# A decoder layer's cross-attention context: joining two token tiles on VectorE before TensorE's sum over partitions, with GpSimd's work of a round put in another order

## Chip, cores and metric

The kernel runs on one NeuronCore of a Trainium2 chip. Its time is the device time of one execution in microseconds (us). The kernel before takes 456.52 us in the median of three runs (455.98 to 457.6).

## What is computed

The reference is one pre-norm decoder layer over 8 batch rows of 256 tokens and 256 features, all in float32. It has three parts, each added to its input: linear self-attention, a cross-attention whose context is one vector for each batch row, and a mixture of 8 experts of which each token takes two. The part that the change touches is the middle one:

```python
def xattn(q, k, v, Wq, Wk, Wv, Wfc):         # k = v = the context, 8 x 256 x 256
    qp = l2norm(q @ Wq)                       # per token, over features
    kp = l2norm(k @ Wk)
    vp = v @ Wv
    kv = jnp.sum(kp * vp, axis=-2, keepdims=True)   # sum over the 256 tokens
    return qp * kv @ Wfc + v
```

The experts' part needs a list of which token goes to which expert. It is made on the chip: each token and choice writes its number and gate into a slot of a table in device memory, and later steps read the table 128 slots at a time.

## The kernel before

**Tiling.** A batch row (`b`, 0 to 7) has 256 tokens, held as T = 2 tiles of 128 partitions, with 256 features along the free axis. Features on partitions come as KD = 2 halves of 128.

**Stages.** The front of the kernel works on rows in a software pipeline. A loop over `i` from 2 to 7 (lines 1072 to 1131) makes one round of each `i`; the round runs stages of row `i` (first norm, queries, keys, context projection), of row `i-1` (self-attention's state, attend, output), of row `i-2` (cross-attention) and of row `i-3` (choice of experts, ranks, table). Rows 0 and 1 have a start written out by hand (lines 1022 to 1069), and rows 6 and 7 an end written out by hand (lines 1135 to 1195), in which the first steps of the experts' matrix products are put between the stages by `meanwhile`. After that only experts' steps are left. A step takes 128 gathered tokens through one expert, some 36 steps in all.

**Order.** TensorE, VectorE, ScalarE and the queue that SyncE issues DMAs from execute in the order of the source. GpSimd's order is chained to the source's by `in_turn` and by the list `behind`. [...] So a stage's place in the loop is its place in every engine's queue, and a wait at the head of a queue holds all that stands behind it.

**The context's sum.** `context` (L388) projects 128 context tokens with `Wk` and `Wv` side by side; ScalarE squares the key half with a running sum (`ssk`), VectorE multiplies the halves (`prod`, L401). After the second tile `inverse_length` computes 1/length on GpSimd: a maximum (L330, tile `l2n_k`) and a power (L309, tile `l2r_k`, named `rn` in the code). `context_sum` (L469) then forms the 256 sums over tokens as matrix products, with `prod` as the weights and the column `rn[:, t]` as the moving operand, accumulated over the two token tiles; a copy by VectorE (L480, `kvc`) takes the result out of PSUM. It shares the PSUM bank of `state` (L453), whose matrix products come before it. `turn_queries` (L556) is the first to use the result, one round later.

**GpSimd's share of a round.** `add_context` (L530) adds the context to the residual for `cross_out`, a 128x512 addition (L536, tile `xc`; in the hand-written end VectorE does it, L534). `residual` (L372) adds the output bias (L374). The two inverse lengths and the inverse roots of the three norms (tiles `rs_a`, `rs`, `rs_b`) are small operations. `place` (L706) ends with four indirect DMAs (L729) that write the table `slots` for one row: two token tiles times two choices.

**Readers of the table.** `fetch_slots` (L850) has SyncE read 128 slots (L853, tile `ids`). In the round `i` = 7 (`i - 3 == RA`) six of these are issued, for steps 3 to 8; in the source they stand behind `place(4)`, and the table is one tensor to the dependency tracker: a read waits for earlier writes, and a write for earlier reads. The gathers of tokens for the experts' steps (`gather`, L871) are GpSimd's too.

Of the kernel before, what the change touches and what calls it, by code (L numbers as in the profile page):

```python
# [13 lines left out]
ALU = mybir.AluOpType  # L14
# [3 lines left out]
P = 128  # L18
# [6 lines left out]
ORDERED = mybir.DependencyInfo(mybir.DependencyClass.NoSync, mybir.DependencyReason.SCHED_ONLY)  # L25
# [4 lines left out]
def decoder_kernel(  # L30
# [34 lines left out]
    nc = tc.nc  # L65
    ctx.enter_context(tc.manual_schedule(engines={ET.PE, ET.SP, ET.DVE, ET.Activation}))
    B, S, D = x.shape
# [3 lines left out]
    T = S // P  # L71
# [16 lines left out]
    slots = dram.tile([NTILE, 2 * P], I32, name="slots")  # L88
# [4 lines left out]
    def ps(name):  # L93
        return psum.tile([P, 512], F32, tag="ps", name=name)
# [4 lines left out]
    def const(name, shape, dtype=F32):  # L99
        return cpool.tile(shape, dtype, tag=name, name=name)  # L100
# [31 lines left out]

    load(0)

    any_w = const("any_w", [P, P])
    nc.vector.memset(any_w, 1.0)
    def idle(n):
        p = ps("idle")
        for _ in range(n):
            nc.tensor.matmul(p[:, 0:P], any_w, any_w, start=True, stop=True)  # L140

    idle(8)
    mhalf = const("mhalf", [P, 2 * T])
# [27 lines left out]
    for i, v in enumerate((gamma, beta)):  # L171
        at = n_b1 + i * KD
# [108 lines left out]
    def gate_row():  # L281
        p = ps("pglog")
        for k in range(KD):
            nc.tensor.matmul(
                p[:, 0:E], beta_w[:, k, :], wg_s[:, k, :], start=(k == 0), stop=(k == KD - 1)
            )
        nc.vector.tensor_copy(glog, p[:, 0:E])


    behind = []  # L290
# [162 lines left out]
    def state(st):  # L453
# [12 lines left out]
            st["kvz"], p, headsx[:, None, :].to_broadcast([P, KD, VW]), ALU.mult  # L466
        )

    def context_sum(st):  # L469

        b = st["b"]
        p = st["pstate"][:, KD * VW : KD * VW + KD]
        for m in range(KD):
            for t in range(T):
                nc.tensor.matmul(
                    p[:, m : m + 1], st["prod"][:, t, m * P : (m + 1) * P], st["rn"][:, t : t + 1],
                    start=(t == 0), stop=(t == T - 1),
                )
        st["kv"] = small.tile([P, KD], F32, tag="kvc", name=f"kvc{b}")
        nc.vector.tensor_copy(st["kv"], p)  # L480

# [134 lines left out]
    puts = []  # L616

    def named(st):

        def new(name, shape, dtype=F32):  # L620
            t = st[name] = small.tile(shape, dtype, tag=name, name=f"{name}{st['b']}")
            return t
        return new
# [82 lines left out]
    def place(st):  # L706

        new = named(st)
        at = st["b"] * T
        hot = st["hot"]  # L710
        slot = new("slot", [P, T, E])
        nc.vector.tensor_tensor(
            slot,
            st["prank"].rearrange("p (t e) -> p t e", e=E),
            slot0[:, None, :].to_broadcast([P, T, E]),
            ALU.add,
        )
        nc.vector.tensor_tensor(
            hot, hot, slot[:, :, None, :].to_broadcast([P, T, 2, E]), ALU.mult
        )  # L720
        pos = new("pos", [P, T, 2])
        nc.vector.tensor_reduce(pos, hot, axis=AX.X, op=ALU.add)
        posi = new("posi", [P, T, 2], I32)
        nc.vector.tensor_copy(posi, pos)
        earlier = list(behind)
        behind.clear()
        for t in range(T):
            for c in range(2):
                put = nc.gpsimd.indirect_dma_start(  # L729
                    out=slot_rows,  # L730
                    out_offset=bass.IndirectOffsetOnAxis(ap=posi[:, t, c : c + 1], axis=0),
                    in_=pay[:, at + t, c, :], in_offset=None,
                )
                tc.declare_no_dep(
                    put.ins, group="slots", reason="every token and choice has a slot of its own"
                )
                tc.add_to_no_dep_group("slots", put.ins)
                for name in earlier:
                    tc.add_manual_dep(put.ins, name, ORDERED, reason="in the order of the source")
                puts.append(put.ins.name)  # L740
                behind.append(put.ins.name)


    w2_s = w2pool.tile([P, E, FC, D], F32, tag="w2", name="w2_s")
# [94 lines left out]
    def said(s, which, engine):  # L839
        top = (E, NTILE)[which] - 1  # L840
        plan, at = (plans["a"], s) if s < NA else (plans["b"], s - NA)
        return nc.values_load(
            plan[0:1, which, at : at + 1], engines=[engine], min_val=0, max_val=top,
            skip_runtime_bounds_check_because=CLAMPED,
        )
# [4 lines left out]
    def fetch_slots(s):  # L850
        q_sp = said(s, 1, ET.SP)
        ids[s] = mpool.tile([P, 2], I32, tag="ids", name=f"ids{s}", bufs=16)
        got = nc.sync.dma_start(ids[s], slot_rows[bass.ds(q_sp * P, P), :])  # L853
        if s in (0, NA):
            for name in puts[0 : RA * T * 2] if s == 0 else puts:
                tc.add_manual_dep(got.ins, name, WRITTEN, reason="all slots are written")

    def fetch_weights(s):
        e_sp = said(s, 0, ET.SP)
        w1s[s] = mpool.tile([P, KD, F], F32, tag="w1", name=f"w1_{s}", bufs=3)  # L860
        nc.sync.dma_start(
            w1s[s], w1_rows[bass.ds(e_sp * D, D), :].rearrange("(k p) f -> p k f", p=P)
        )
        b2s[s] = mpool.tile([P, D], F32, tag="b2", name=f"b2_{s}", bufs=3)
        nc.sync.dma_start(b2s[s], b2_flat[bass.ds(e_sp * D, D)].partition_broadcast(P))
# [5 lines left out]
    def gather(s):  # L871
        xgs[s] = mpool.tile([P, D], F32, tag="xg", name=f"xg{s}", bufs=6)
        in_turn(nc.gpsimd.indirect_dma_start(  # L873
            out=xgs[s][:, :], out_offset=None, in_=rows_d[0 : reach(s), :],
            in_offset=bass.IndirectOffsetOnAxis(ap=ids[s][:, 0:1], axis=0),
        ))
# [129 lines left out]
    def step_end():  # L1006

        at = len(done)
        while len(done) == at:
            next(work)  # L1010
# [4 lines left out]
    def run(stage, b, *args):  # L1015
        if 0 <= b < B:
            stage(rows[b], *args)
# [29 lines left out]


    run(state, 0)
    run(lift_queries, 1)  # L1050
    run(keys, 1, 0)
    run(context_sum, 0)
# [19 lines left out]
    for i in range(2, B):  # L1072
        run(turn_context, i)
        run(turn_normed, i)
        run(choose, i - 3)
        run(state, i - 1)
        run(turn_second, i - 2)
        run(powers, i - 3, False)
        run(add_context, i - 2)
        run(gates, i - 3)  # L1080
        run(first_stats, i + 1)
        run(queries, i)
        run(residual, i)
        run(cross_queries, i - 2)
        run(context_sum, i - 1)
        run(lift_queries, i)
        run(rank, i - 3)
        run(attend, i - 1)
        run(place, i - 3)
        run(first_norm, i + 1)  # L1090
        run(attended, i - 1)
        if i - 3 == RA - 1:
            plan = plan_steps("a", RA - 1, NA, full_tiles)
            next(plan)
        if i - 3 == RA:
            for s in range(3, NA):
                fetch_slots(s)
        run(turn_queries, i - 2)
        run(keys, i, 0)
        if i == 2:  # L1100
            gate_row()
        run(cross_out, i - 2)
        if i == B - 1:
            gather(0)
            gather(1)
        if i - 3 == RA - 1:
            next(plan)
        run(turn_attended, i - 1)
        run(keys, i, 1)
        run(key_powers, i)  # L1110
        run(last_norms, i - 2)
        if i - 3 == RA - 1:
            for _ in plan:
                pass
            for s in range(3):
                fetch_slots(s)
        run(attention_out, i - 1)
        run(second_stats, i - 1)
        run(lift_keys, i)
        run(base, i - 2)  # L1120
        run(context, i, 0)
        run(turn_last, i - 2)
        run(second_norm, i - 1)
        run(context, i, 1)
        run(logits, i - 2)
        if i + 3 < B:
            load(i + 3)
        for e in seconds[i]:
            load_second(e)
        if i - 3 == RA - 1:  # L1130
            fetch_weights(0)
# [3 lines left out]
    p, q = B - 2, B - 1  # L1135
    run(choose, p - 1)
    run(state, q)
    run(turn_second, p)
    run(powers, p - 1, True)
    run(gates, p - 1)  # L1140
    turn(0)
    fetch_weights(1)
    run(cross_queries, p)
    run(rank, p - 1)
    run(context_sum, q)
    meanwhile(0.8)
    run(attend, q)
    run(place, p - 1)
    run(attended, q)
    run(add_context, p, True)  # L1150
    run(turn_queries, p)
# [19 lines left out]
    run(rank, p)  # L1171
    run(gates, p)
    run(place, p)
    run(add_context, q, True)
    holding[0] = True
    meanwhile(1.7)
# [13 lines left out]
    meanwhile(3.5)  # L1190
    run(rank, q)
    run(place, q)
    step_end()
    for _ in plan_steps("b", B - 1, NSTEP - NA, other_tiles):
        pass
# [50 lines left out]
```

## Time and profile before

| what | value |
|---|---|
| median of 3 runs | 456.52 us (455.98 to 457.6) |
| profiled execution | 460.37 us, of which the span from first to last instruction is 458.7 us |
| mean granted TensorE clock | 0.983 |
| busy: TensorE, weight loads, VectorE, ScalarE, GpSimd | 435.1, 374.2, 186.5, 212.3, 187.3 us |
| one round of the loop, from the transposes of row 4's context (94.81 us) to those of row 5's (115.55 us) | 20.74 us |
| `context_sum` in all: matrix products, weight loads (L475) | 64 of 7.7 us; 64 of 8.3 us |
| additions by GpSimd, 128x512: `xc` (L536), bias (L374) | 6 of 1.28 us each; 8 of 1.27 us each |
| table writes (L729), issue by GpSimd | 32 of 1.01 us each, 32.2 us in all, with 9.0 us of idle time before them |

"Busy" is the time in which an engine's instructions run; a matrix product's end is modelled. In a row of the profile the first number is the start in us from the span's start or, in a group, the sum; the bracket behind a row tells how long the engine was idle and what ended that. PE is TensorE's products, PEld its weight loads, DVE VectorE, ACT ScalarE, POOL GpSimd, SPq the queue of SyncE. A float32 product of the source is two in the trace.

### The profile page before, as it was taken

Reading aid. Unit: us, or ns where it says so; the run is one execution under the profiler, and the core shown is the slowest. Engines: PE = TensorE matmul, PEld = TensorE weight load, DVE = VectorE, ACT = ScalarE, POOL = GpSimd, SP = SyncE. Lnnn points to the kernel's source line nnn. Section 1 sums busy time; section 2 is a strip of 40 time slices with the busy share of each in tenths; the row PEclk is TensorE's granted clock in tenths of the full one; section 3 lists DMA queues with packets and bytes.
Section 4 is the critical chain, followed back from the end, with each engine's and each line's share of the span. In section 5 each row is a group of like instructions: output and inputs, shape, how many; then the busy total and the mean of one; then the engine's idle time right before and its main releaser. Section 6 shows DMA issues by size and latency. Waiting matters only on the chain. (4 is left out here: it accounts for less than half of the span.)

```text
span 458.7 us, 8535 instructions
## 1 busy us (share of the span) xinstructions
PE 435.1 (95%) x2679; PEld 374.2 (82%) x2679; DVE 186.5 (41%) x692; ACT 212.3 (46%) x551; POOL 187.3 (41%) x201
## 2 busy tenths in 40 slices
PE   9999999999999999997999999999999999999960
PEld 7568777686878688886999999999999999999950
DVE  1776878787897867361112121111212111121100
ACT  4545546555644455343444444444444444444420
POOL 7323363645546662744342433324243342422220
PEclk9999999999999999998999999999999999999995
DMA  8603268584404256886777667686776767677325
GB/s 228 210 25 115 73 204 111 170 190 126 94 24 129 46 150 228 136 204 118 189 199 236 164 218 191 201 239 152 228 186 202 194 195 238 156 224 197 70 30 191
DMA packets 48368, 74.37 MB, mean 162 GB/s; under 512 B 9773, under 2 KB 37810, under 8 KB 48290
## 3 DMA queue, kind: packets, MB, share of 16 engines
q1 hardware_dynamic: 39298, 63.10, 44.8%
q0 software_dynamic: 8208, 9.91, 14.3%
q10 hardware_dynamic: 816, 0.79, 0.5%
q8 instruction: 24, 0.39, 0.3%
q14 instruction: 22, 0.18, 0.2%
HBM read 64.44 MB, written 11.44 MB: 165 GB/s over the span
## 5 line engine op out<-in xcount | busy, mean ns | idle before, releaser
L902 PEld LDWEIGHTS ph<-xgT,w 128*128 128x128 f32 x1152 | 170.0, 192 | 17.1 <-issue 4.2
L902 PE MATMUL ph<-xgT,w 128*128 128x128 f32 x1152 | 176.1, 276 | 3.3 <-issue 3.2
L906 ACT ACTIVATE hT<-ph,vcols 128x128 f32<-128x128 f32 x288 | 105.3, 367 | 141.8 <-PE ph L902 118.0
L915 PE MATMUL py<-w_s,hT 128*128 x576 | 170.8, 382 | 0.0
L936 POOL DMA_INDIRECT acc<-yg,ids x36 | 57.1, 1586 | 152.5 <-DVE yg L930 129.7
L885 DVE TENSOR_SCALAR xgT<-pt,vcols 128x128 f32<-128x128 f32 x72 | 26.2, 406 | 157.1 <-PE pt L882 156.7
L915 PEld LDWEIGHTS py<-w_s,hT 128*128 128x128 f32 x576 | 88.7, 193 | 0.6
L873 POOL DMA_INDIRECT xg<-rows_d,ids x36 | 36.0, 1001 | 11.2 <-issue 9.6
L930 DVE SCALAR_TENSOR_TENSOR yg<-py,ids,b 128x256 f32<-128x256 f32 x36 | 17.4, 484 | 45.8 <-ACT hT L906 35.5
L729 POOL DMA_INDIRECT slots<-pay,posi x32 | 32.2, 1006 | 9.0 <-issue 8.0
L347 PE MATMUL pxkv<-xwkv_s,cT 128*128 128x512 f32 x64 | 30.1, 593 | 0.0
L347 PE MATMUL pkv<-wkv_s,hT 128*128 128x512 f32 x64 | 29.9, 593 | 0.0
L347 PEld LDWEIGHTS pxkv<-xwkv_s,cT 128*128 128x128 f32 x64 | 11.5, 190 | 8.0 <-issue 7.6
L924 ACT ACTIVATE b<-b,ids 128x256 f32<-128x256 f32 x36 | 17.9, 498 | 0.0
L347 PEld LDWEIGHTS pkv<-wkv_s,hT 128*128 128x128 f32 x64 | 11.1, 190 | 8.2 <-issue 8.1
L309 POOL TENSOR_TENSOR rs_b<-ve_b,mhalf 128x2 f32<-128x2 f32 x8 | 8.2, 1021 | 23.1 <-DVE ve_b L322 23.1
L309 POOL TENSOR_TENSOR rs_a<-ve_a,mhalf 128x2 f32<-128x2 f32 x8 | 5.7, 708 | 27.1 <-DVE ve_a L322 27.1
L347 PEld LDWEIGHTS po<-wo_s,turnedoT 128*128 128x128 f32 x64 | 12.1, 190 | 4.6 <-issue 3.3
L347 PE MATMUL pq<-xwq_s,turnedx2T 128*128 128x256 f32 x64 | 15.2, 381 | 0.5 <-issue 0.5
L511 ACT COPY turnedoT<-pto 128x512 f32<-128x512 f32 x8 | 4.7, 585 | 23.6 <-PE pto L341 21.0
L410 PE MATMUL pq<-hT,wq_s 128*128 128x256 f32 x64 | 15.2, 381 | 0.2 <-ACT hT L386 0.2
L347 PE MATMUL pfc<-xwfc_s,turnedq2T 128*128 128x256 f32 x64 | 15.2, 380 | 0.0
(193 smaller groups left out, 523.2 us busy)
## 6 DMA issues: line engine op xcount, KB each, us to landing
w<-in_L_ffn_W_dram SPq DMA_DIRECT2D x36, 1024.0 KB
w_s<-in_L_ffn_W_dram SPq DMA_DIRECT2D x8, 1024.0 KB
b<-in_L_ffn_b_dram SPq DMA_DIRECT2D x36, 128.0 KB
x<-in_x_dram SPq DMA_DIRECT2D x8, 256.0 KB
rows_d<-h SPq DMA_DIRECT2D x8, 256.0 KB
acc<-x SPq DMA_DIRECT2D x8, 256.0 KB
c<-in_ctx_dram SPq DMA_DIRECT2D x7, 256.0 KB
ids<-slots SPq DMA_DIRECT2D x36, 1.0 KB
```

The costliest lines, as they stand in the source:

```text
L309: in_turn(nc.gpsimd.tensor_tensor(dst, src, mhalf[:, 0:n], ALU.pow))
L347: nc.tensor.matmul(p[:, 0:width], srcT[:, k, t * P : (t + 1) * P], w[:, k, 0:width], start=(k == 0), stop=(k == KD - 1),)
L410: nc.tensor.matmul(p[:, m, :], wq_s[:, k, m * P : (m + 1) * P], st["hT"][:, k, :], start=(k == 0), stop=(k == KD - 1),)
L729: put = nc.gpsimd.indirect_dma_start(out=slot_rows, out_offset=bass.IndirectOffsetOnAxis(ap=posi[:, t, c : c + 1], axis=0), in_=pay[:, at ...
L873: in_turn(nc.gpsimd.indirect_dma_start(out=xgs[s][:, :], out_offset=None, in_=rows_d[0 : reach(s), :], in_offset=bass.IndirectOffsetOnAxis ...
L885: nc.vector.tensor_scalar(ready[s][:, k, :], p[:, k * P : (k + 1) * P], gamma_c[:, k : k + 1], beta_c[:, k : k + 1], op0=ALU.mult, op1=ALU ...
L902: nc.tensor.matmul(p, w1s[s][:, k, c * P : (c + 1) * P], ready[s][:, k, :], start=(k == 0), stop=(k == KD - 1),)
L906: nc.scalar.activation(hT[:, c, :], p, AF.Gelu_apprx_tanh, bias=vcols[:, bass.ds(e_act * FC + c, 1)],)
L915: nc.tensor.matmul(p[:, 0:D], hidden[s][0][:, c, :], w2_flat[:, bass.ds((e_pe * FC + c) * D, D)], start=(c == CHUNKS[0]), stop=(c == CHUNK ...
L924: nc.scalar.activation(b2s[s], b2s[s], AF.Copy, scale=gate_of(s))
L930: nc.vector.scalar_tensor_tensor(yg, p[:, 0:D], gate_of(s), b2s.pop(s), op0=ALU.mult, op1=ALU.add)
L936: in_turn(nc.gpsimd.indirect_dma_start(out=acc[0 : reach(s), :], out_offset=bass.IndirectOffsetOnAxis(ap=ids.pop(s)[:, 0:1], axis=0), in_= ...
```

## The change

A new stage `add_tiles` scales the first product tile by its inverse lengths and adds the second tile times its own, both on VectorE, in place. `context_sum` then needs one product for each half of the features instead of two, with a column of ones (the constant that the idle products at the start used, renamed) as the moving operand.

Stages are moved with it. In the loop `add_tiles` comes straight behind `state`; `context_sum` moves from behind `cross_queries` to before it; `add_context` moves from behind `powers` to behind `lift_queries`, and so, in GpSimd's queue, from behind the context's inverse length to behind the queries' one. The four table writes become a stage `put`: the writes of the first token tile stand behind `place`, those of the second behind `cross_out`, and in the last round (`i` = 7) behind `second_stats`. In the hand-written end `add_tiles` stands before `powers`, and `context_sum` before `cross_queries`.

```diff
+    def add_tiles(st):
+        prod, rn = st["prod"], st["rn"]
+        nc.vector.tensor_scalar_mul(prod[:, 0, :], prod[:, 0, :], rn[:, 0:1])
+        nc.vector.scalar_tensor_tensor(
+            prod[:, 0, :], prod[:, 1, :], rn[:, 1:2], prod[:, 0, :], op0=ALU.mult, op1=ALU.add
+        )
...
         for m in range(KD):
-            for t in range(T):
-                nc.tensor.matmul(
-                    p[:, m : m + 1], st["prod"][:, t, m * P : (m + 1) * P], st["rn"][:, t : t + 1],
-                    start=(t == 0), stop=(t == T - 1),
-                )
+            nc.tensor.matmul(
+                p[:, m : m + 1], st["prod"][:, 0, m * P : (m + 1) * P], ones[:, 0:1],
+                start=True, stop=True,
+            )
...
+    def put(st, *ts):            # the indirect DMAs that ended place()
+        at, posi = st["b"] * T, st["posi"]
         earlier = list(behind)
         behind.clear()
-        for t in range(T):
+        for t in ts or range(T):
...
     run(state, 0)
+    run(add_tiles, 0)
...
         run(state, i - 1)
+        run(add_tiles, i - 1)
         run(turn_second, i - 2)
         run(powers, i - 3, False)
-        run(add_context, i - 2)
         run(gates, i - 3)
         run(first_stats, i + 1)
         run(queries, i)
         run(residual, i)
+        run(context_sum, i - 1)
         run(cross_queries, i - 2)
-        run(context_sum, i - 1)
         run(lift_queries, i)
+        run(add_context, i - 2)
         run(rank, i - 3)
         run(attend, i - 1)
         run(place, i - 3)
+        run(put, i - 3, 0)
...
         run(cross_out, i - 2)
+        if i + 1 < B:
+            run(put, i - 3, 1)
...
         run(second_stats, i - 1)
+        if i + 1 == B:
+            run(put, i - 3, 1)
...
     run(state, q)
     run(turn_second, p)
+    run(add_tiles, q)
     run(powers, p - 1, True)
     run(gates, p - 1)
     turn(0)
     fetch_weights(1)
+    run(context_sum, q)
     run(cross_queries, p)
     run(rank, p - 1)
-    run(context_sum, q)
     meanwhile(0.8)
     run(attend, q)
     run(place, p - 1)
+    run(put, p - 1)
```

More of the change, by code (lines that the diff above doesn't have):

```diff
@@ L133, in decoder_kernel @@
     load(0)
-    any_w = const("any_w", [P, P])
-    nc.vector.memset(any_w, 1.0)
+    ones = const("ones", [P, P])
+    nc.vector.memset(ones, 1.0)
     def idle(n):
@@ L139, in idle @@
         for _ in range(n):
-            nc.tensor.matmul(p[:, 0:P], any_w, any_w, start=True, stop=True)
+            nc.tensor.matmul(p[:, 0:P], ones, ones, start=True, stop=True)
     idle(8)
@@ L724, in place @@
         nc.vector.tensor_copy(posi, pos)
+    def put(st, *ts):
+        at, posi = st["b"] * T, st["posi"]
         earlier = list(behind)
         behind.clear()
-        for t in range(T):
+        for t in ts or range(T):
             for c in range(2):
-                put = nc.gpsimd.indirect_dma_start(
+                ins = nc.gpsimd.indirect_dma_start(
                     out=slot_rows,
@@ L732, in place @@
                     in_=pay[:, at + t, c, :], in_offset=None,
-                )
[L734 to L737, printed above, removed]
+                ).ins
+                tc.declare_no_dep(
+                    ins, group="slots", reason="every token and choice has a slot of its own"
+                )
+                tc.add_to_no_dep_group("slots", ins)
                 for name in earlier:
-                    tc.add_manual_dep(put.ins, name, ORDERED, reason="in the order of the source")
-                puts.append(put.ins.name)
-                behind.append(put.ins.name)
+                    tc.add_manual_dep(ins, name, ORDERED, reason="in the order of the source")
+                puts.append(ins.name)
+                behind.append(ins.name)
     w2_s = w2pool.tile([P, E, FC, D], F32, tag="w2", name="w2_s")
@@ L1173, in decoder_kernel @@
     run(place, p)
+    run(put, p)
     run(add_context, q, True)
@@ L1192, in decoder_kernel @@
     run(place, q)
+    run(put, q)
     step_end()
```

## Prediction

> **What bounds the kernel now.** I read the page first, then busy time by stretches of one round, then the timeline of one round, last the timeline around the round `i` = 7 and the start of the hand-written end.
>
> ```profile
> PE 435.1 (95%) x2679; PEld 374.2 (82%) x2679; DVE 186.5 (41%) x692; ACT 212.3 (46%) x551; POOL 187.3 (41%) x201
> 83.00:104.00 21.00, 20.75 (x108) 15.46 (x107) 16.56 (x66) 11.67 (x30) 11.31 (x14) 1.00 0.67 164
> ```
>
> The second line is one round: TensorE (first number behind the length) is busy 20.75 of 21.00 us, VectorE 16.56, GpSimd 11.31. TensorE is the bound in the rounds and in the experts' steps, so each microsecond that TensorE loses or saves there moves the end. The next fence is the middle of the round of `i` = 5.
>
> ```profile
> 96.02 1.28 POOL L536 TENSOR_TENSOR xc<-x,c 128x512 f32<-128x512 f32 x1
> 96.22 1.11 DVE L645 TENSOR_TENSOR ex<-m 128x16 f32<-128x16 f32 x1
> 98.16 0.43 DVE L465 TENSOR_TENSOR kvz<-pstate,headsx 128x272 f32<-128x272 f32 x1
> 100.55 0.95 PE L475 MATMUL pstate<-l2r_k,prod 128*128 128x1 f32 x8
> 101.36 0.17 PE L698 MATMUL prank<-before,ones_h 128*128 128x16 bf16 x1
> 101.53 0.16 DVE L480 COPY kvc<-pstate 128x2 f32<-128x2 f32 x1 [0.92 <-PE pstate L475]
> 101.75 0.38 PE L490 MATMUL pat<-kvz,qT 128*128 128x136 f32 x1 [0.20 <-DVE kvc L480]
> 104.31 0.81 ACT L561 ACTIVATE turnedq2T<-ptq,kvc 128x256 f32<-128x256 f32 x2
> 104.83 0.19 PEld L347 LDWEIGHTS pfc<-xwfc_s,turnedq2T 128*128 128x128 f32 x1 [0.24 <-ACT turnedq2T L561]
> ```
>
> Three things are to be seen. The context's sum holds TensorE from 100.55 to the next product at 101.36: 0.81 us for 8 products, 0.10 each. VectorE's L645 takes 1.11 us while GpSimd adds `xc` and ends 0.03 us after it; the same instruction takes 0.15 us at 158.48 with no addition beside it. And TensorE is released by VectorE's `kvc` (0.20 us of idle) and, with 0.06 us to spare, by ScalarE's `turnedq2T`, whose first half ends at 104.77. The last place is where the loop meets its end:
>
> ```profile
> 149.01 0.96 POOL L729 DMA_INDIRECT slots<-pay,posi  x1 [0.30 <-issue]
> 154.07 4.55 SPq L853 DMA_DIRECT2D ids<-slots  x6
> 155.12 1.08 POOL L309 TENSOR_TENSOR rs_b<-ve_b,mhalf 128x2 f32<-128x2 f32 x1 [0.37 <-DVE ve_b L322]
> 157.29 0.21 POOL L330 TENSOR_SCALAR l2n_k<-ssk 128x2 f32<-128x2 f32 x1 [1.09 <-ACT junkk L398]
> 157.59 0.72 POOL L309 TENSOR_TENSOR l2r_k<-l2n_k,mhalf 128x2 f32<-128x2 f32 x1
> 158.51 0.38 PE L882 MATMUL pt<-ident,xg 128*128 128x128 f32 x2
> 159.35 1.99 PE L347 MATMUL pq<-xwq_s,turnedx2T 128*128 128x256 f32 x8 [0.46 <-issue]
> 159.51 0.43 DVE L465 TENSOR_TENSOR kvz<-pstate,headsx 128x272 f32<-128x272 f32 x1
> DMA packets 199, 0.06 MB, mean 96 GB/s; under 512 B 144, under 2 KB 199, under 8 KB 199
> DMA packets 194, 0.20 MB, mean 326 GB/s; under 512 B 3, under 2 KB 194, under 8 KB 194
> SPq L853 <- DMA slots<-pay,posi: 13.9, 3, 10.9
> 210.50:213.90 3.40, 3.10 (x12) 2.82 (x13) 0.56 (x2) 0.98 (x3) 0.64 (x1) 0.52 0.89 60
> ```
>
> The last of row 4's four table writes is issued at 149.01. SyncE's six reads of the table wait for it until 154.07 (10.9 us is the longest wait of that line), 5.1 us after that issue. They are issued one every 0.84 us, the sixth at 158.29. The two DMA lines are the stretches 159.2 to 159.8 and 159.8 to 160.4: small packets, which the reads consist of, end with the first, so the last read has landed at about 160. Row 7's `l2n_k` and `l2r_k` run meanwhile, since nothing of the table stands before them in GpSimd's queue. The last line is for the clock, below.
>
> **The change, part by part.** Times are on the clock of the trace before.
>
> *TensorE's products.* 4 of 8 go in each of 8 rows: 4 x 0.10 = 0.40 us a row. `kvc` is now long done when `pat` comes, so its 0.20 us of idle can go too: up to 0.6 us a row.
>
> *VectorE's additions.* `add_tiles` is a TENSOR_SCALAR on 128x256 (nearest row: L313, 0.41 us) and a SCALAR_TENSOR_TENSOR with two operands in SBUF (L449, of that kind, takes 0.685 us at 512 elements; rows of 256 elements with two operands, L401, take 0.42). The second reads the first's result: about 0.8 us a row. In the rounds `i` = 3 to 6, L645 gets 0.96 us back as `xc` leaves, so `kvz` ends at 96.9 to 97.7 and `add_tiles` at about 98.5. TensorE ends `queries` at 98.8. No wait; the cover is L645's lost stall, and without it TensorE would wait 0.7 us.
>
> *GpSimd's order.* Here a rule speaks against the change. The row: L645, with both inputs in SBUF, waits for a 128x512 addition; L424, L501 and L435, with one input in PSUM, don't. The Trainium skill, GPSIMD Engine Reference, section Key points, says that GpSimd shares its SBUF interfaces with VectorE and that contention comes with two SBUF inputs and with VectorE's two-port modes, so single-input copies and scalings too. By the row, the bias addition (now 101.2 to 102.5, since VectorE gets to `rs_a` a little earlier) meets `place`'s product L718, which has two SBUF inputs and comes at 101.6 now that `kvc` no longer waits 0.92 us: it ends at 102.5, and `off`, ScalarE's norm and `turnedq2T` come 0.27 us earlier than before, not 0.6. By the rule also the reciprocals L500 wait, for `xc` at its new place (about 104.0 to 105.3), up to 1.3 us; no row here has one beside such an addition. `o` then ends at 105.7 instead of 104.92, and its transpose begins at 106.77: covered, so the sum is the same. The bound is L561: TensorE's gain stops at 0.3 us a round. Bounds: 0 and 0.6. Rounds 3 to 6: 4 x -0.3 = -1.2 us. Round 2 has no choice of experts and 0.4 us of work between: -0.4 us. Row 0: VectorE's queue to `o` (26.1) is TensorE's limit at 26.4, and the added 0.8 us meets 0.83 us of waits there: -0.1 us.
>
> *The table writes of the second tile* stand behind `rs` in the rounds up to 6: two issues, 1.1 + 0.3 + 1.0 us, from 110.5 to 113.0, before `rs_b` at 113.3. Nothing else waits; cost nothing, with 0.3 us of cover. In round 6 they delay the reads for steps 0 to 2 (137.77) by 2 to 3 us, and weights behind them on SP's queue that TensorE needs at 162: covered.
>
> *Round 7.* VectorE is late here, behind the list of steps that round 6 makes (L788 and others): L645 runs at 138.87, not 0.7 us earlier as in a usual round, and waits for the bias addition, which now comes where `xc` was, to 139.25; L649's 1.14 us stall behind it goes. `kvz` at 140.1, `add_tiles` from 140.4 to 141.3. TensorE is ready for the sum at 140.34: it waits 0.95 us, and is 0.35 us later at `pat` after the products saved and the `kvc` wait. +0.4 us.
>
> *The hold.* In this round the second tile's writes stand behind `second_stats`, while SyncE's six reads stand before them. GpSimd's queue becomes: `rs_b`, write 3, write 4, `l2n_k`, `l2r_k`. Write 3 has to wait until all six reads have landed, as they read the same table, and the reads wait for write 2. With pq2 1.4 us later, `l2r_q` ends at 146.2, `xc` 147.5; writes 1 and 2 are issued at 147.7 and 149.1. Reads from 149.1 + 5.1 to 5.5 = 154.4, the sixth at 158.6, landed at 160.4 (its 1.7 us as before). GpSimd, ready at 156.5, stands for 4 us. Then write 3 and 4 (1.1 + 0.3 + 1.0 + 0.3) to 163.1, `l2n_k` and `l2r_k` (0.3 + 0.7) to 164.2, `add_tiles` (0.8, at the head of VectorE's queue, which it holds) to 165.1. TensorE is done with `turn(0)` at 159.1, and its next instruction is now the sum: it idles 6 us. All experts' products and the last rows' stages stand behind it. Before, its idle time there was 0.62 us (158.73 to 159.35). `cross_queries` starts at 165.5, 6.15 us later, of which 0.35 is round 7's; 0.9 us of products is saved behind `prank`. +4.9 us.
>
> *The clock.* The last line of the fence: after two gaps of 1.9 and 2.1 us at 206 to 210.8, the granted clock is 0.52 for 3.4 us. A gap of 6 us should do the same where TensorE is the bound: 3.4 x 0.48 = +1.6 us. The skill (TensorE: Matmul & The Clock Gate, section HAM oscillation) puts the limit at one idle window of about 3.4 us and the return at a busy one; with the windows badly placed that is two at half rate, 3.3 us. The row is this kernel's own, so 1.6; 0 and 3.3 are the ends.
>
> **Sum:** -0.1 - 0.4 - 1.2 + 0.4 + 4.9 + 1.6 = +5.2 us. The profiled execution took 460.37 us (span 458.7), so 465.6 for a profiled one; the runs shown stand 3.85 us below it at a median of 456.52, and the same difference gives 461.7 us.
>
> **Rivals.**
>
> *GpSimd is not held (not slower).* If the sixth read lands before `rs_b` ends (156.5), write 3 goes at once, its two issues end at 159.1 and `l2r_k` at 160.2, `add_tiles` at 161.0: TensorE waits 1.9 us, 1.3 more than before, less 0.9. Clock untouched. With 0.6 us in each of five rounds, -3.0 - 0.1 + 0.4 + 0.4 = -2.3 us: 454.2. For it: the fetches may be faster than 0.84 us with fewer writes ahead. Against: six issues alone take 4.2 us. 7%; with the usual gains of 0.3, about 455.6 us.
>
> *The hold is longer.* In rounds 3 and 4 the second write landed 9 and 10 us after its issue, beside weight loads, where the later rounds have 5 to 5.7 (the semaphores' updates in the trace). If row 4's takes 9, the reads start 3 to 4 us later and TensorE with them; with two slow clock windows +10 us: 466.5. 18%.
>
> *Every round loses.* If `add_tiles` meets a GpSimd operation and TensorE waits 0.7 us in each of five rounds, nothing is gained there: 5 x (0.7 - 0.3) on top of the hold, +9 us: 465.5. For it: VectorE at 16.6 of 21 us; against: GpSimd is idle from 96.1 to 100.5. 10%.
>
> *As worked out*, 65%: 459 to 464.
>
> **How the numbers follow.** Predicted 461.7 us. The range 457.8 to 466.5 takes in full gains with no slow clock at its low end, the long hold at its high end. 0.3% (1.4 us) is about what a measurement of this kernel can tell from no change. Slower by more than that: the last three cases, less a small part of the first of them: 0.90. Of the 7% and what is over, faster 0.05, no change 0.05.
>
> **What would show it.** Right: in the new trace `l2r_k` of row 7 starts several us after row 7's `ssk`, behind two table writes; VectorE's first `add_tiles` instruction of that row waits for GpSimd; TensorE has one gap of about 6 us near 157 to 163, with a clock near 0.5 after it; L645's group falls from 0.66 us mean to near 0.2; L718's rises; a round takes 20.2 to 20.6 us. Wrong: no gap over 3 us at the start of the end, or rounds longer than 20.7 us.

## The result, and the profile after

The changed kernel takes 462.11 us in the median of four runs (461.92 to 463.55), the kernel before on the same chip 456.38 us (455.98 to 457.6): a ratio of 1.0142, 95% interval 1.0118 to 1.0166 (the two medians alone give 1.0126, inside it). On another chip, later, the same pair stood at 1.0168 (1.0141 to 1.0196). The forecast was 461.7 us.

The profiled execution took 461.92 us, with a span of 460.1, so it lies 0.19 us below its median, where the profiled one of before lay 3.9 us above. Before's profile holds the dip at 206 to 213.9 us that the prediction showed (3.4 us at a clock of 0.52; its two gaps are 1.47 and 1.70 us between products, while the 1.9 and 2.1 us of the prediction are those of the weight loads); the profile after has none there. So the spans differ by only 1.4 us while the medians differ by 5.7: the two traces are compared stage by stage here, not by their spans.

First the round `i` = 5 in the timeline of the kernel after (start, duration, engine, line; the bracket is the idle time before and what ended it). Lines have moved: `ex` is now L652, `add_tiles` L472 and L473, the sum L482, `place`'s product L725, `xc` L543, `turnedq2T` L568, the table writes L740, the reads L864.

```profile
93.92 0.15 DVE L652 TENSOR_TENSOR ex<-m 128x16 f32<-128x16 f32 x1
95.68 0.48 DVE L473 SCALAR_TENSOR_TENSOR prod<-prod,l2r_k 128x256 f32<-128x256 f32 x1
96.52 0.50 PE L482 MATMUL pstate<-ones,prod 128*128 128x1 f32 x4
98.93 1.28 POOL L374 TENSOR_TENSOR x<-x,bo_b 128x512 f32<-128x512 f32 x1
99.24 1.01 DVE L725 TENSOR_TENSOR hot<-hot,slot 128x32 f32<-128x32 f32 x1
101.42 1.27 POOL L543 TENSOR_TENSOR xc<-x,c 128x512 f32<-128x512 f32 x1
101.68 0.25 DVE L507 RECIPROCAL den<-den 128x16 f32<-128x16 f32 x1
101.77 0.81 ACT L568 ACTIVATE turnedq2T<-ptq,kvc 128x256 f32<-128x256 f32 x2
102.28 1.99 PE L347 MATMUL pfc<-xwfc_s,turnedq2T 128*128 128x256 f32 x8 [0.20 <-ACT turnedq2T L568]
```

The sum holds TensorE for 0.36 us (96.52 to the next product at 96.88) instead of 0.81. `ex` is back at 0.15 us, and `add_tiles` ends at 96.16, ahead of the sum. The stall has moved: L725 takes 1.01 us beside the bias addition; before, as L718, it took 0.19:

```profile
102.59 0.19 DVE L718 TENSOR_TENSOR hot<-hot,slot 128x32 f32<-128x32 f32 x1
```

TensorE no longer waits for `kvc` but for ScalarE's `turnedq2T`. The transposes of the context (`ptc`), which open each round, stand at 52.20, 72.37, 92.52 and 112.67 us, against 53.35, 74.09, 94.81 and 115.55: a round takes 20.16 us instead of 20.73. When the round `i` = 7 begins, TensorE is 3.26 us ahead (before, then after):

```profile
136.34 0.64 PE L341 MATMUL ptc<-ident,c 128*128 128x128 f32 x4
133.08 0.64 PE L341 MATMUL ptc<-ident,c 128*128 128x128 f32 x4
```

Then the round `i` = 7 and the start of the hand-written end, from the same timeline (SPq is SyncE's DMA queue; its duration is from the first of six issues to the last):

```profile
138.44 0.61 PE L482 MATMUL pstate<-ones,prod 128*128 128x1 f32 x4 [1.19 <-DVE prod L473]
146.27 0.97 POOL L740 DMA_INDIRECT slots<-pay,posi  x1 [0.30 <-issue]
152.77 4.55 SPq L864 DMA_DIRECT2D ids<-slots  x6
159.66 1.04 POOL L740 DMA_INDIRECT slots<-pay,posi  x1 [6.30 <-DMA ids<-slots]
162.33 0.73 POOL L309 TENSOR_TENSOR l2r_k<-l2n_k,mhalf 128x2 f32<-128x2 f32 x1
163.09 0.35 DVE L472 TENSOR_SCALAR prod<-prod,l2r_k 128x256 f32<-128x256 f32 x1 [5.99 <-POOL l2r_k L309]
164.02 1.01 PE L482 MATMUL pstate<-ones,prod 128*128 128x1 f32 x4 [7.97 <-DVE prod L473]
164.90 3.76 PE L347 MATMUL pq<-xwq_s,turnedx2T 128*128 128x256 f32 x8
```

Read the brackets upward from the sum at 164.02: TensorE stood 7.97 us for `add_tiles`, which stood 5.99 us for `l2r_k`, which came behind two table writes, of which the first stood 6.30 us for the six reads. The last line takes 3.76 us; at full clock it took 1.99. The stretches of that stage show why (length, TensorE's busy time and count, and after ScalarE's and GpSimd's numbers the granted clock):

```profile
157.00:163.00 6.00, 0.00 (x0) 0.00 (x0) 0.10 (x1) 0.00 (x0) 2.92 (x4) 0.81 0.74 231
163.00:166.40 3.40, 2.38 (x8) 2.11 (x9) 2.78 (x13) 0.00 (x0) 1.22 (x2) 0.50 0.96 116
166.40:170.00 3.60, 3.60 (x15) 2.97 (x14) 0.72 (x4) 1.27 (x5) 0.00 (x0) 0.50 0.08 16
```

TensorE runs nothing at all from 157 to 163, and everything behind that at half rate. The next stretch, 170.00 to 173.40, has a clock of 0.86. Counted as time at 0.50 that is 2.3 us inside the gap (6 x 0.19 / 0.5), then 3.4, 3.6 and 0.95 us (3.4 x 0.14 / 0.5): 10.2 us in all, where the prediction had 3.4.

### The profile page after: what moved, and what is told of

It is laid out like the page before. It is cut to its first block, busy times and chain, and to the rows that moved or that the text cites. A ratio compares the mean times of both kernels' runs of the same rounds, so it can differ in the third digit from the quotient of the medians.

```text
span 460.1 us, 8471 instructions
## 1 busy us (share of the span) xinstructions
PE 432.6 (94%) x2647; PEld 371.6 (81%) x2647; DVE 189.6 (41%) x708; ACT 212.3 (46%) x551; POOL 187.7 (41%) x201
## 5 line engine op out<-in xcount | busy, mean ns | idle before, releaser
L740 POOL DMA_INDIRECT slots<-pay,posi x32 | 32.5, 1016 | 16.6 <-issue 7.4
L347 PE MATMUL pq<-xwq_s,turnedx2T 128*128 128x256 f32 x64 | 17.5, 421 | 0.0
L347 PEld LDWEIGHTS pfc<-xwfc_s,turnedq2T 128*128 128x128 f32 x64 | 11.7, 190 | 5.4 <-ACT turnedq2T L568 3.6
L347 PEld LDWEIGHTS po<-wo_s,turnedoT 128*128 128x128 f32 x64 | 12.1, 190 | 4.6 <-issue 3.3
L347 PE MATMUL po<-wo_s,turnedoT 128*128 128x256 f32 x64 | 15.2, 380 | 0.0
```

The source lines that it names most:

```text
L347: nc.tensor.matmul(p[:, 0:width], srcT[:, k, t * P : (t + 1) * P], w[:, k, 0:width], start=(k == 0), stop=(k == KD - 1),)
L740: ins = nc.gpsimd.indirect_dma_start(out=slot_rows, out_offset=bass.IndirectOffsetOnAxis(ap=posi[:, t, c : c + 1], axis=0), in_=pay[:, at ...
```

## The experiments

The theory: the rounds gain 3.3 us; the second tile's late table writes of round 7 hold GpSimd and through it TensorE; the long gap halves the clock; and the sum's early place in the end exposes what is late. The rivals are given with each run. All ratios are to the kernel before, measured on the same chip in the same set. The kernel after itself was run beside e9 and e10 only; a difference between its ratio and that of another experiment, or between e1's and those of e5 and e6, is one between chips.

**e1: both tiles' writes early.** The hold is taken out, all else of the change stays.

```diff
-        run(put, i - 3, 0)
+        if i + 1 < B:
+            run(put, i - 3, 0)
+        else:
+            run(put, i - 3)
...
-        if i + 1 == B:
-            run(put, i - 3, 1)
```

> Only change against the kernel after: in the round i = 7 both tiles' table writes of row 4 are issued behind `place`, as before; `add_tiles`, the halved sum and every other move stay. Theory (the late writes hold GpSimd, and through `l2r_k`, `add_tiles` and the sum TensorE): the wait of the write for the six reads is gone, TensorE's gap at the start of the end shrinks from 7.97 us to 1 to 2 us, the granted clock stays near 1 there. The rounds keep their 3.3 us (TensorE is 2.84 us early at the first `turn`), of which 1 to 1.5 us go into the remaining wait less the 0.9 us of products saved: 453.5 to 455. Rival (the sum's place ahead of `cross_queries` and the two additions are what costs, whatever the writes do): TensorE still idles over 4 us there and the time stays at 459 or above.

Measured: 459.72 us, ratio 1.0013 (0.9992 to 1.0035). On this chip the kernel before takes 458.67 us, so on the scale of the expectation that is 457.0, between the theory and the rival. So the hold accounts for most of the loss, but the forecast of a clear gain was wrong. In e1's trace (TensorE's sum in the round `i` = 7, then GpSimd, VectorE and TensorE's sum in the end):

```profile
139.50 0.61 PE L482 MATMUL pstate<-ones,prod 128*128 128x1 f32 x4 [1.21 <-DVE prod L473]
156.37 0.73 POOL L309 TENSOR_TENSOR l2r_k<-l2n_k,mhalf 128x2 f32<-128x2 f32 x1
159.09 0.43 DVE L465 TENSOR_TENSOR kvz<-pstate,headsx 128x272 f32<-128x272 f32 x1
159.82 0.48 DVE L473 SCALAR_TENSOR_TENSOR prod<-prod,l2r_k 128x256 f32<-128x256 f32 x1
160.35 0.61 PE L482 MATMUL pstate<-ones,prod 128*128 128x1 f32 x4 [2.44 <-DVE prod L473]
```

`l2r_k` is there at 157.10, but `add_tiles` comes 2.3 us later. VectorE does not idle there: it works through the choice of experts from 157.09 and through `kvz`, and reaches `add_tiles` behind them. TensorE waits 2.44 us for a busy VectorE. Behind it, the experts' first products wait 0.98 us for ScalarE. The single executions of e1 go from 457.39 us at a mean granted clock of 0.988 to 463.19 at 0.977; the profiled one shows no slow stretch after its gap. Five executions each have a clock of 0.988: their median is 457.54 us in e1 and 457.98 in the kernel before, so the waits alone take nearly all that the rounds gain, and the slower clock of the other executions comes on top.

**b2: the late write alone, in the kernel before** (the writes are split off `place` as in the change; that part isn't shown).

```diff
...
+        if i + 1 < B:
+            run(put, i - 3)
+        else:
+            run(put, i - 3, 0)
...
         run(second_stats, i - 1)
+        if i + 1 == B:
+            run(put, i - 3, 1)
```

> The kernel before with one edit: in the round i = 7 the second tile's two table writes stand behind `second_stats`; the sum keeps its 8 products and its place behind `rank`. Theory (the hold costs what reaches TensorE): GpSimd stands 3 to 5 us as in the kernel after and `l2r_k` ends at about 161 to 163 instead of 158.3, but the sum comes only at about 161.4, so TensorE waits 0 to 2 us: 456.5 to 458.5. Rival (the hold costs its full length wherever the sum stands, since experts' steps hang on the same queue): 461 to 464.

Measured: 461.54 us, ratio 1.0056 (1.0038 to 1.0074), on the same chip as e1: 2.6 us more than before, somewhat above what was expected (up to 2.1 us more) and well below the rival (4.6 us or more). From its trace, which runs 2.2 us late from the first rows on, behind a stretch at 18 to 22 us with a clock of 0.55 to 0.60 that the edit has no part in:

```profile
160.91 1.04 POOL L732 DMA_INDIRECT slots<-pay,posi  x1 [2.54 <-DMA ids<-slots]
164.37 1.05 PE L475 MATMUL pstate<-l2r_k,prod 128*128 128x1 f32 x8 [0.83 <-POOL l2r_k L309]
```

GpSimd is held 2.54 us (3 to 5 expected) and TensorE waits only 0.83 us, since the sum stands behind `cross_queries` and `rank` there. A wait of 1.25 us for `turnedoT` further on is most of the rest. The late write costs about 2.6 us with the sum behind, and, by after against e1, 5.9 us (1.0142 less 1.0013, times 456.4) with the sum ahead and the slow clock behind the gap.

**e3: after, with the sum of the end behind `rank`.**

```diff
-    run(context_sum, q)
     run(cross_queries, p)
     run(rank, p - 1)
+    run(context_sum, q)
```

> The kernel after with the hand-written end's `context_sum` moved back behind `cross_queries` and `rank`; the late writes stay. Theory: GpSimd is held as long, TensorE does 2.2 us of products first and then idles 5 to 6 us instead of 8, so the time falls by about 2.2 us, to 459.5 to 460.5; the clock falls as before, for it is still a long gap. Rival (all of the loss is the clock's, which a gap of 5 us sets off as much as one of 8): within 0.7 us of 462.1.

Measured: 464.62 us, ratio 1.0106 (1.0052 to 1.016). That is 1.6 us less than the 1.0142 of after by the middle of a wide interval, but the medians of its own set give 1.0130, no less than after's 1.0126: the time of e3 decides nothing. Its trace shows the mechanism:

```profile
163.85 1.01 PE L482 MATMUL pstate<-ones,prod 128*128 128x1 f32 x4 [5.20 <-DVE prod L473]
```

The gap at the sum is 5.20 us instead of 7.97, as expected, and the clock still halves: 0.59, 0.50 and 0.50 in the three stretches of 3.4 us from 160.4 on. The rival is not excluded by e3.

**e4, e7 and e9: the hold kept, the clock kept up.** Idle products fill the gap.

```diff
+    idle(48)            # e4; 24 in e7, 34 in e9
     run(context_sum, q)
```

> The kernel after with 48 products of 128x128 into an unused bank put in front of the end's `context_sum`, 5.3 us of work for TensorE inside the gap of 8 us; they end before `add_tiles` does, so nothing waits for them. It prices the clock alone. Theory with the clock of the prediction (one window at half rate): 1.6 us less, 460.5. With what the trace after suggests (two windows): 3.0 to 3.4 us less, 458.7 to 459.1, and `pq` at 1.99 us instead of 3.76. If the clock costs nothing there: 462.1.

e4 measured 465.55 us, ratio 1.0145 (1.0096 to 1.0193), and left the question open: the 48 products took 10.88 us, 0.227 us each and not 0.11, and the sum came at 166.75, though `add_tiles` had ended at 163.64.

> As e4, with 24 products in place of 48: in e4 they took 10.88 us, 0.227 us each, and ended 2.8 us after `add_tiles`. 24 take 5.4 us and end near 161.5, 2.5 us before `add_tiles` ends, so only the clock is changed. Theory (clock near half rate for two windows, 2.4 to 3.4 us): 1.007 to 1.009 of the kernel before, against 1.0142 for the kernel after. By the prediction's 1.6 us: 1.0107. If the clock costs nothing: 1.014.

e7 measured 462.15 us, ratio 1.0145 (1.0118 to 1.0173): a miss. Its profiled execution, the fastest at 460.81 us, keeps the clock at 1.00 in that stage; the others have mean clocks of 0.982 to 0.985. A gap of 2.51 us was left. That it sets off the slow clock in those executions is likely by their clocks, but their traces are not there to show the place.

> As e7, with 34 products: at the measured 0.227 us they fill 7.7 us and end at about the same time as `add_tiles`, so neither a gap nor a delay is left; e7 still left TensorE a gap of 2.51 us, and e1, with one of 2.44 us, showed granted clocks from 0.977 to 0.988 over its executions. Theory (half rate after the gap costs two windows, and a gap of 2.5 us costs one in some executions): 2.4 to 3.4 us less than e11, which is the kernel after on the same chip, and a granted clock of 0.985 or more in every execution. If the clock is worth nothing: within 0.7 us of e11.

> The kernel after, unchanged, beside e9 on one chip: 1.012 to 1.016 of the kernel before, granted clock 0.976 to 0.980.

e9 measured 460.35 us, ratio 1.0113 (1.0093 to 1.0134); e11, the kernel after beside it, 462.66 us, ratio 1.0168 (1.0141 to 1.0196). The difference is 2.3 us. Five of e9's six executions have a clock of 0.987 to 0.989, all of e11's 0.974 to 0.979. The first product behind the sum, in e9 and then in e11:

```profile
164.95 1.97 PE L347 MATMUL pq<-xwq_s,turnedx2T 128*128 128x256 f32 x8
```

```profile
165.51 3.76 PE L347 MATMUL pq<-xwq_s,turnedx2T 128*128 128x256 f32 x8
```

So the clock costs 2.3 us of the loss: just under the bottom of the range that was expected for two windows (2.4), and over one (1.6). The traces agree. This is the cross-attention's last product (`pfc`) in e9, in e11 and in the profile of after:

```profile
172.75 1.89 PE L347 MATMUL pfc<-xwfc_s,turnedq2T 128*128 128x256 f32 x8
175.10 1.89 PE L347 MATMUL pfc<-xwfc_s,turnedq2T 128*128 128x256 f32 x8
174.59 1.89 PE L347 MATMUL pfc<-xwfc_s,turnedq2T 128*128 128x256 f32 x8
```

From the sum (164.48, 164.63 and 164.02) that is 8.27, 10.47 and 10.57 us: 2.2 and 2.3 us for the clock.

**e6: `add_context` back at its old place** (in e1).

```diff
         run(powers, i - 3, False)
+        run(add_context, i - 2)
...
-        run(add_context, i - 2)
```

> The kernel e1 with GpSimd's `add_context` back at its old place in the rounds, behind `powers`, so that the 128x512 addition runs beside VectorE's `ex` product again. Theory (the addition must leave for `add_tiles` to be in time): `ex` takes 1.1 us again, `add_tiles` ends 0.96 us later, against 0.4 us of slack in front of TensorE's sum, so TensorE waits 0.5 to 0.7 us in each of the rounds 3 to 6: 2 to 2.8 us more than e1, 1.0055 to 1.0075 of the kernel before. Rival (that move is not needed; the products saved are what counts): within 0.002 of e1.

Measured: 462.15 us, ratio 1.0134 (1.0094 to 1.0174), more than twice the loss that was expected against e1. The rival is out. From its trace, the round `i` = 5, then the sum of the round `i` = 7 and the two stretches behind it:

```profile
96.53 1.12 DVE L652 TENSOR_TENSOR ex<-m 128x16 f32<-128x16 f32 x1
99.74 0.61 PE L482 MATMUL pstate<-ones,prod 128*128 128x1 f32 x4 [0.45 <-DVE prod L473]
102.66 1.12 DVE L725 TENSOR_TENSOR hot<-hot,slot 128x32 f32<-128x32 f32 x1
105.81 1.99 PE L347 MATMUL pfc<-xwfc_s,turnedq2T 128*128 128x256 f32 x8 [0.32 <-ACT turnedq2T L568]
143.86 1.01 PE L482 MATMUL pstate<-ones,prod 128*128 128x1 f32 x4 [2.37 <-DVE prod L473]
143.80:147.20 3.40, 3.34 (x10) 2.90 (x11) 1.58 (x9) 0.00 (x0) 0.00 (x0) 0.50 0.85 246
147.20:150.60 3.40, 3.40 (x17) 2.94 (x16) 1.58 (x8) 1.43 (x5) 0.44 (x2) 0.53 0.45 178
```

The wait at the sum is 0.45 us, as expected. But VectorE now meets two additions in a round, `xc` at `ex` and the bias at L725, each for about 1.1 us, and `turnedq2T` is late again behind them (0.32 us). A round takes 21.08 us, longer than before's 20.73: without that move each round loses, as one rival of the prediction had it. The loss beyond the forecast goes with the clock: behind the wait of 2.37 us in the round `i` = 7 it is 0.50 and 0.53 for 6.8 us (last two lines), and behind the end's sum 0.54 for 3.4 us more. Five of the six executions have mean clocks of 0.977 to 0.981; the sixth, at 0.988, took 458.22 us, 1.0063 of before's median and so inside the forecast.

**e5: the sum behind, in round 7 and in the end** (in e1).

```diff
-        run(context_sum, i - 1)
+        if i + 1 < B:
+            run(context_sum, i - 1)
         run(cross_queries, i - 2)
+        if i + 1 == B:
+            run(context_sum, i - 1)
...
-    run(context_sum, q)
     run(cross_queries, p)
     run(rank, p - 1)
+    run(context_sum, q)
```

> The kernel e1 (both tiles' writes early) with the sum moved back behind `cross_queries` in the round i = 7, and behind `cross_queries` and `rank` in the hand-written end; `add_tiles` and the halved products stay everywhere. In e1 VectorE, late with the choice of experts, makes TensorE wait 1.21 us for `add_tiles` in round 7 and 2.44 us at the start of the end. Theory (those two waits are what eats the rounds' 3.3 us): both go, 3 us less than e1 of which up to 1 us comes back as a wait for the experts' first step: 0.994 to 0.997 of the kernel before. Rival (what TensorE saves before the end is lost again in the experts' steps, which wait for weights or gathers): 1.000 or above.

Measured: 451.77 us, ratio 0.9917 (0.9893 to 0.9941), better than expected. Both waits at the sum are gone; the longest gap at the start of the end is now 0.91 us, for the experts' first input. By the ratios it gains 4.4 us on e1, of which the two gaps in e1's trace, 1.21 and 2.44 us less the 0.46 that is left for `turnedx2T`, explain 3.2; the rest fits the clock, 0.986 to 0.990 in all six executions where e1's went down to 0.977.

**e8 and e10: what binds the rounds.** e8 is e5 with `first_norm` behind `turn_queries`; e10 is the kernel before with that move alone.

```diff
-        run(first_norm, i + 1)
         run(attended, i - 1)
...
         run(turn_queries, i - 2)
+        run(first_norm, i + 1)
```

> The kernel e5 with one more move in the rounds: `first_norm` (VectorE's `off`, ScalarE's two L367 instructions of 0.55 us each) stands behind `turn_queries`, so that ScalarE makes `turnedq2T` before it. It prices the bound of the rounds. Theory (TensorE is 1.05 us early at `ptq` of each round, and `turnedq2T`, which waits behind `h` on ScalarE, cuts that to 0.58): up to 0.47 us more in each of the rounds 3 to 7, 1.9 to 2.4 us less than e5. Rival (another wait stands right behind, for `o` or for `h` of the next row): within 0.5 us of e5.

> The kernel before with only `first_norm` behind `turn_queries`, the edit that set e8 apart from e5 (0.48 us a round there). In the kernel before TensorE reaches `pfc` 0.5 us after `turnedq2T`'s first half is made, so by the theory that ScalarE binds the rounds only once the products are saved, this move alone gives nothing: within 0.6 us of the kernel before. Rival (ScalarE binds the rounds of before too): 1.4 us or more less.

e8: 450.67 us, ratio 0.9913 (0.988 to 0.9947); e10: 455.34 us, ratio 0.9996 (0.9988 to 1.0003). In e8's trace, the round `i` = 5:

```profile
99.42 0.84 ACT L568 ACTIVATE turnedq2T<-ptq,kvc 128x256 f32<-128x256 f32 x2
100.94 1.89 PE L347 MATMUL pfc<-xwfc_s,turnedq2T 128*128 128x256 f32 x8
```

Its first half is made 1.1 us ahead (99.42 + 0.42 against 100.94), TensorE's wait is gone, and a round takes 19.69 us instead of 20.16. That holds for the rounds `i` = 3 to 5; round 6 takes 20.40 us in both, so 1.4 us came where 1.9 to 2.4 were expected. The medians differ by 1.1 us, and their intervals overlap, so the gain over e5 is shown by the trace and not by the times. In e10 the same move gives nothing: before, ScalarE was not what bound the rounds.

## Why the prediction was right

By the ratios, the 1.42% falls into three parts: the products saved and the new order of the rounds gain 0.83% (e5; 3.8 us); the sum's early place in round 7 and in the end, with the slower clock of some executions, costs 0.96% (e1 less e5; 4.4 us); the late writes of round 7, the clock included, cost 1.29% (after less e1; 5.9 us). Each ratio has an interval of about 0.2 to 0.25% either way, so each part is good to about 1.5 us; the medians of the sets give 3.6, 4.7 and 4.7 us. The late writes of the rounds up to 6, put at nothing by the prediction, are in e5's part and were not run alone. The prediction's time held, and its path with it; its terms missed in both directions, and that their sum came out is luck.

- *Rounds 2 to 6: -1.6 us by the prediction, -2.8 us by the trace* (0.74, then 0.57, 0.57, 0.59 and 0.38 us a round). The mechanism was right: `ex` lost its stall, the bias addition met L725, and `turnedq2T` came 0.25 us earlier against the round's start (0.27 predicted). The size was off: the prediction read "0.06 us to spare" from the weight load at 104.83, which `turnedq2T` releases. The product itself, in the profile before, began only at 105.25, so 0.5 us were to spare:

```profile
105.25 1.89 PE L347 MATMUL pfc<-xwfc_s,turnedq2T 128*128 128x256 f32 x8
```

  e10 shows that slack, e8 that the bound comes right behind it.
- *The port, row against rule.* The row was followed, and in the rounds it decided right: L725 with two SBUF inputs waited; the reciprocal L507, with one, takes 0.25 us wholly beside `xc`. But this does not speak against the rule. The section that the prediction cites names VectorE's two-port modes, not the reciprocal, and other operations with a single tensor to read were held. Two scalings and the addition from the profile before, then an addition and a copy from e6:

```profile
34.38 0.22 DVE L276 TENSOR_SCALAR gwg<-wg_s,vcols 128x8 f32<-128x8 f32 x1
34.65 1.33 DVE L276 TENSOR_SCALAR gwg<-wg_s,vcols 128x8 f32<-128x8 f32 x1
34.67 1.27 POOL L536 TENSOR_TENSOR xc<-x,c 128x512 f32<-128x512 f32 x1
140.54 1.27 POOL L374 TENSOR_TENSOR x<-x,bo_b 128x512 f32<-128x512 f32 x1
140.55 1.29 DVE L654 CAST fi<-i 128x4 f32<-128x4 uint32 x1
```

  The scaling takes 0.22 us ahead of `xc` and 1.33 beside it, the copy 0.16 in the median of its eight and 1.29 here. The prediction's row was too narrow.
- *Row 0: -0.1 predicted, -0.44 measured. Round 7: +0.4 predicted, +0.42 measured* (TensorE waits 1.19 us instead of 0.95; it is earlier there).
- *The hold: +4.9 predicted, about +7 measured.* The path was right, the length mis-sized: TensorE stood 7.97 us, not 6. The predicted 165.5 us for `cross_queries` is on the clock of the trace before and leaves out the 1.7 us that row 0 and the rounds were to gain, so it stands for 163.8 in the new trace; measured: 164.90, although TensorE came in 1.5 us earlier than predicted. Against before's 159.35 that is 5.55 us late, from a lead of 2.84: 8.4 us, or 7.5 less the 0.9 us of products saved, as the prediction counts; 0.5 of it is the sum at half rate. From write 2 to the first read took 6.5 us (5.1 to 5.5 predicted), and from the sixth issue at about 157.0 to write 3 took 2.7 us (1.7). In the traces of the other runs the first of these times goes from 3.9 us (e1, from write 4) to 6.7 (e11, from write 2); what sets it is not shown.
- *The clock: +1.6 predicted, 2.3 measured* (e9 against e11). The row of this kernel, one window, was followed, and is 0.7 us short; the rule of the Trainium skill (TensorE: Matmul & The Clock Gate, section HAM oscillation), weighed as two windows, gave 3.3 and is 1.0 us over. In e11 the slow time is again 10.2 us (clocks of 0.68, 0.50 and 0.58 over 157 to 163, to 166.4 and to 170: 3.8, 3.4 and 3.0). 5.5 of it had passed when the sum began at 164.63, and the other 4.7 at half rate make 2.4. In the profile of after only 3.3 us of it had passed, which by the same working makes 3.4; the trace has 2.3 there too. On that way TensorE waits 0.98 us for ScalarE's `hT` at full clock (e9) and 0.18 in after, so part of the slow time falls where TensorE would have waited.
- *The sum of the terms.* As measured, -2.84 us up to the end of round 7, +7.0 for the hold without the slow clock and +2.3 for the clock make +6.5 us, as the ratio has it (the medians: 5.7); the prediction had -1.3, +4.9 and +1.6. The gain and the loss were both taken too small, and no mechanism ties the two errors to each other.
- *Rival "not held".* e1 comes closest to that case, and the prediction gave it 454.2 us. It measured 1.0013, no gain. The figure left out VectorE: `add_tiles` is late there even without the hold.
- *Rival "every round loses".* It needed the addition of `xc` to stay where it was: e6.

## What to carry to other kernels

Before a write to a shared table is moved behind another stage, list the readers that have been issued ahead of it and are still waiting for earlier writes: the write waits for their landing, and everything on its engine's queue with it. A saving on the bound engine reaches the end only if what feeds it is early at every place where the new consumer stands: the halved sum with its new order was worth 3.8 us in e5 and nothing in e1, which differ only in where two of the eight sums stand. When a slack is read from a trace, read it at the product and not at its weight load. When VectorE's work is put beside an addition of GpSimd's, look for rows of scalings and copies too: here some were held as long as products of two tensors.

## What was not expected

- The clock after short gaps. Gaps of 2.44 us in e1's profiled execution and of 2.51 in e7's left the granted clock at 1.00; in e6's, one of 2.37 us was followed by 0.50 and 0.53 over 143.8 to 150.6, and one of 1.88 by 0.54 over 167.2 to 170.6; over the executions of e1 the mean clock runs from 0.977 to 0.988. A gap of about 2 us is a lottery there; with one of 8 us all ten executions of the kernel after have mean clocks of 0.974 to 0.980.
- A float32 product of 128x128 with a 128-wide moving operand, back to back in one bank, took 0.227 us in e4 (10.88 us for 48).
- The load of the context two rounds ahead (SyncE, L125) waits 47.4 us in all for `xc` after the change, against 17.5 before (longest 12.1 against 4.4), since `xc` is made later in the round. No wait of TensorE follows from it in the trace.
